# A two-layer metaformer on one core: products of ones before the first scans, layernorm sums in one PSUM bank, another conv input layout, ordered spreads and new planner keys

## The chip, the cores and the metric

The kernel runs on one core of one Trainium2 chip. The metric is device time in microseconds (us); the time before is the median of three runs. The profile is of one execution of the kernel before.

## The reference, cut to what matters

The input `x` is (8, 384, 32, 32) in float32. Two layers follow; every layernorm is without weights.

```python
# layer 0
x = x + mamba(ln_c(x))          # selective state space, 768 channels, 16 states, 1024 tokens
t = tokens(x); t = t + ffn0(ln_t(t)); x = image(t)
# layer 1
x = x + displaced_gauss(ln_c(x))  # each 8 channels shifted, then a 5x5 gaussian
t = tokens(x); t = t + ffn1(ln_t(t)); x = image(t)

def mamba(s):
    xin, z = split(s @ in_proj.T)
    u = silu(causal_conv3(xin) + conv_b)
    dt, Bm, Cm = split(u @ x_proj.T)
    dt = softplus(dt @ dt_proj.T + dt_b)
    h_t = exp(dt_t * A) * h_{t-1} + (dt_t * u_t) * B_t     # A = -exp(A_log)
    y_t = sum_n h_t * C_t + D * u_t
    return (y * silu(z)) @ out_proj.T

def ffn(x):                     # for images 0 to 4 only; zero for 5 to 7
    W = sign(W - mean) per 5 groups of output rows   # straight-through form
    h = gelu(quant(x @ W1.T + b1)); return quant(h @ W2.T + b2)
    # quant: scale by 128 / max|.| of the image and clip
```

## The kernel before, in words

One image is 1024 tokens, worked on in two halves of 512 (`s`), so the state space part has 16 units (8 images x 2 halves), `units`. Channels lie on the 128 partitions. A unit has 6 channel blocks `j` of 128, and each block has 4 state groups `g` of 4 states: 24 scan steps a unit, 384 in all.

**One scan step** (`scan`, L847 to L935): POOL multiplies the spread `dt*u` (`dus`) with B into a buffer `t` (L868, twice, 128x1024 each); ACT writes exp(dt*A) from the spread `dt` (`dts`) into PSUM (L878, four times); DVE runs four scans of 512 (L893); POOL multiplies one half by C (L914), DVE the other (L927); PE sums both over the states into the PSUM tile `y` by four products with 32 output columns each (L935). There are five buffers `t`, and PE's sum is what gives one back. `prep` makes softplus on ACT (L824) and `dt*u` on POOL (L837) for two blocks; `spread` copies each through DRAM (`via`) and back with 8 DMAs of 128 KB, which repeat each channel group over the partitions: two buffers `p`, four quarters `q` each.

**Beside the scans** lie, for the next unit, the load of x, its layernorm, the input product (`xin`, `in_proj`, L645), the three-tap convolution on DVE (L676) and `x_proj` (L760); and for units already done the output product (`end`, L997), both feed-forward nets (`ffn`, products L1386 and L1465) and `conv`, the shifted gaussian. `binarize` prepares the four weight matrices in the first part of the run (Sign on ACT at L1126). `early` makes the first layernorm and z of the last six units ahead of time.

**Layernorm** (`layernorm`, L491) is called 52 times and needs two sums over the 384 channels a call, so `total` (L458) runs 104 times. Before, `total` makes three products with a 128x32 block of ones, each into its own 32 rows of one PSUM bank (L464); ACT copies the 96 rows to SBUF (L477); and a product with `pick` (ones in one row of each 32) adds the three and spreads the sum over 128 rows (L484).

**Conv** (`conv`, L1546): per image, both halves are normalized and DVE transposes them in 32x32 blocks into `xt` (L1569); per 128 channels PE applies the vertical taps (`ups`, two products of 256 columns for each half, L1601), DVE transposes (L1615), PE applies the horizontal taps (`overs`, four products of 128 columns, L1629), DVE transposes again (L1642), and POOL adds the input (L1652). `ups` reads `xt` with 32 floats from one element to the next.

**Order.** Each step is an `op` with an engine, a planned duration and a key. `Flow.run` plays the program forward with these durations and, whenever an engine is free, takes the ready step of the lowest key (a step that needs another ACT table costs `PEN` more, and `HOLD` delays it). What comes out is a fixed order on each engine; on the chip each engine runs its own list in order and waits for semaphores. All DMAs are issued by SP in its own fixed order, and each waits for the eighth one before it. The keys are counted in scan steps: `ROWS`, `CONVS`, `K..`, `A..`, `EZ..` are shifts for parts of the work, and `UNITS` has four more for each unit (of `prep`, of the next unit's load and layernorm, of its `xin` and `x_proj`, and of `end`), all zero before.

Before, the constant `FILL` of 1e9 turns `gaps` off, which finds holes in PE's list before 45 us (`FIRST`) of the played time.

Of the kernel before, what the change touches and what calls it, by code (L numbers as in the profile page):

```python
# [36 lines left out]

KB, KE, KC_, KY, KG = -0.73, 4.53, 0.68, -3.95, -25.21  # L40

KP, KR = -4.7, 10.49
KEND, KZ, KL, KX, KXP = 1.3, 23.33, -31.97, -2.16, -4.45

KI, KJ = 196.21, 703.54
EZ, EZ0, EZ1 = 6, -56.93, 53.6

AP, AD, AA, AL = 41.75, -45.76, -50.69, -258.62

PEN = 8.61  # L50

GBS = 260.0


ROWS = [
    [15.34, -7.72, -143.06, 131.51, -3.17, 59.74, -84.96, -78.05],
    [94.3, 121.48, 131.64, -65.6, 211.87, 125.27, 265.88, 164.43],
    [164.72, 212.1, 341.92, 181.75, 145.72, 247.03, 303.52, 178.27],
    [227.6, 313.23, 335.93, 52.96, 178.3, 308.14, 239.43, 298.28],
    [299.47, 295.45, 361.88, 314.75, 306.17, 351.8, 603.44, 450.53],  # L60
]
CONVS = [
    [202.4, 111.11],
    [759.94, 953.69],
    [430.57, 41.38],
]


UNITS = [
    [0.0, 0.0, 0.0, 0.0],  # L70
    [0.0, 0.0, 0.0, 0.0],
    [0.0, 0.0, 0.0, 0.0],
    [0.0, 0.0, 0.0, 0.0],
    [0.0, 0.0, 0.0, 0.0],
    [0.0, 0.0, 0.0, 0.0],
    [0.0, 0.0, 0.0, 0.0],
    [0.0, 0.0, 0.0, 0.0],
    [0.0, 0.0, 0.0, 0.0],
    [0.0, 0.0, 0.0, 0.0],
    [0.0, 0.0, 0.0, 0.0],  # L80
    [0.0, 0.0, 0.0, 0.0],
    [0.0, 0.0, 0.0, 0.0],
    [0.0, 0.0, 0.0, 0.0],
    [0.0, 0.0, 0.0, 0.0],
    [0.0, 0.0, 0.0, 0.0],
]


# [58 lines left out]
OVER = {"PE": 0.0, "DVE": 0.085, "ACT": 0.1, "POOL": 0.05, "SP": 0.0}  # L147
TIE = 0
RUSH = -40.0
FILL, MARGIN, FIRST = 1e9, 0.8, 45.0  # L150
IDLE, COLD = 2.5, 5.0


class Flow:
# [1 line left out]


    SWITCH = 1.5
    HOLD = {"exp": 0.0, "silu": 8.77, "gelu": 2.31, "softplus": 0.0}

    def __init__(self, nc):
        self.nc, self.ops, self.key, self.filler = nc, [], 0.0, None
# [200 lines left out]
def metaformer_flow(ctx, tc, x, mw, f0, offset, f1, out):  # L363
# [24 lines left out]
    op("POOL", 2.0, lambda e: make_identity(nc, ident.ap), (), [ident])  # L388


    pick = one("pick", [P, P])

    def first_rows(e):
        e.memset(pick.ap, 0.0)
        for q in range(Q):
            e.memset(pick.ap[q * D : q * D + 1, :], 1.0)

    op("POOL", 1.0, first_rows, (), [pick])


    mm = ring("mm", [P, T], 3, ps, ordered=False)
    y_r = ring("y", [P, T], 1, ps)
# [55 lines left out]
    def total(src, acc, sq):  # L458

        def chunks(eng):
            for k in range(KC):
                eng.matmul(  # L464
                    acc.ap[k * D : (k + 1) * D, :],
                    ones.ap[:, :D],
                    src.ap[:, k, :],
                    start=True,
                    stop=True,
                    tile_position=(0, k * D),  # L470
                )

        op("PE", 1.0, chunks, [ones, src], [acc], hold=[sq])
        op(
            "ACT",
            0.6,
            lambda eng: eng.copy(sq.ap[: KC * D, 0, :], acc.ap[: KC * D, :]),  # L477
            [acc],
            [sq],
        )  # L480
        op(
            "PE",
            1.0,
            lambda eng: eng.matmul(  # L484
                acc.ap, pick.ap[: KC * D, :], sq.ap[: KC * D, 0, :], start=True, stop=True
            ),
            [pick, sq],
            [acc],
        )

    def layernorm(tn, e):  # L491

# [69 lines left out]
    def load_x(i):  # L562
# [4 lines left out]
            return  # L567
        dma(lambda: t.ap, lambda: halves(x[b], s), (), [t], 768)

    fl.key = -60  # L570
    load_x(0)
    dma(lambda: cw.ap, lambda: conv_w.rearrange("(j p) t -> p j t", p=P), (), [cw], 10)

    def small(dst, src):
# [211 lines left out]

    def spread(src, r):

        via = via_r.new()
        dma(lambda: via.ap, lambda: src.ap, [src], [via])  # L790
        dst = [r.new(Q), r.new(Q)]
        for p in range(2):
            for q in range(Q):
                dma(
                    lambda p=p, q=q: dst[p].ap[q * D : (q + 1) * D],
                    lambda p=p: via.ap.rearrange("(c d) t -> d c t", d=D)[:, 2 * p : 2 * p + 2, :],
                    [via],
                    [dst[p][q]],
                    128,
                )  # L800
        return dst

    def prep(i, a):
# [204 lines left out]
    def state_space():  # L1008
        def at(i, j, g=0.0):
            fl.key = i * UNIT + j * NG + g  # L1010

        fl.key = -50
        ln(0)
        n0 = len(fl.ops)
        for j in range(JC):
            xin(0, j)
        weights.extend([o for o in fl.ops[n0:] if o.eng == "SP"][-1:])
        x_proj(0)
        n0 = len(fl.ops)
        load_bc(0, 0)  # L1020
        fl.key = -48
        prep(0, 0)
        started.extend(o for o in fl.ops[n0:] if o.eng == "SP" and o.key == -48)
        fl.key = -46
        n0 = len(fl.ops)
        for g in range(1, NG):
            load_bc(0, g)
        fl.key = -5
        zin(0, 0)
        zin(0, 1)  # L1030
        loads.extend(o for o in fl.ops[n0:] if o.wait == 0 or o.key == -46)
        for i in range(len(units)):
            nxt = i + 1 if i + 1 < len(units) else None
            for j in range(JC):
                for g in range(NG):
                    scan(i, j, g)
                    at(i, j, g)
                    if g == NG - 1 and j % 2 and i * JC + j + 1 < len(units) * JC:
                        fl.key += KP + UNITS[i][0]
                        prep(*divmod(i * JC + j + 1, JC))  # L1040
                        at(i, j, g)
                    if j == 0 and i > 0 and g == 0:
                        fl.key += KEND + UNITS[i][3]
                        end(i - 1)
                        at(i, j, g)
                    if j == 0 and g in (0, 2):
                        fl.key += KZ
                        zin(i, 2 + g)
                        zin(i, 3 + g)
                        fl.key -= KZ  # L1050
                    if nxt:
                        if j == 1 and g == 0:
                            fl.key += KL + UNITS[i][1]
                            load_x(nxt)
                            if nxt < LATE:
                                ln(nxt)
                            at(i, j, g)
                        if j in (2, 3, 4) and g in (0, 1):
                            fl.key += KX + UNITS[i][2]
                            xin(nxt, 2 * (j - 2) + g)  # L1060
                            at(i, j, g)
                        if j == 4 and g == 2:
                            fl.key += KXP + UNITS[i][2]
                            x_proj(nxt)
                            at(i, j, g)
                        if j == JC - 1:
                            load_bc(nxt, g)
                        if j == JC - 1 and g == 1:
                            fl.key += KZ
                            zin(nxt, 0)  # L1070
                            zin(nxt, 1)
                            fl.key -= KZ
                fl.key = i * UNIT + j * NG + NG + KG
                gate(i, j)
        end(len(units) - 1)


    def binarize(w, dst, kc, o):
# [6 lines left out]
        for g in range(NQ):  # L1085
# [40 lines left out]
                lambda e, z=z, s=s: e.activation(s.ap[:, :flat], z.ap[:, :flat], AF.Sign),  # L1126
                [z],
                [s],
            )
            op(  # L1130
                "POOL",
# [414 lines left out]
    def conv(src, dst, dst_ap):  # L1546

        xt = [hb_r.new(2) for _ in range(KC)]
        for s in range(NS):
# [14 lines left out]
            for c in range(KC):  # L1564
# [2 lines left out]
                    "DVE",  # L1567
                    0.7,
                    lambda e, c=c, tn=tn, ys=ys: e.transpose(  # L1569
                        xt[c].ap.rearrange("p (y c) -> p y c", c=32)[:, ys, :],  # L1570
                        tn.ap[:, c, :].rearrange("p (y x) -> p y x", x=32),
                    ),
                    [tn],
                    [xt[c][s]],
# [1 line left out]
        for c in range(KC):  # L1576
# [18 lines left out]
            for h in range(2):  # L1595
                acc = mm.new()

                def ups(e, lt=lts[0], acc=acc, h=h, c=c):
                    for k in (0, 1):
                        cs = slice(h * 16 + k * 8, h * 16 + k * 8 + 8)  # L1600
                        e.matmul(  # L1601
                            acc.ap.rearrange("p (c y) -> p c y", y=32)[:, k * 8 : k * 8 + 8, :],
                            lt.ap[:, 2 * h + k, :],
                            xt[c].ap.rearrange("p (y c) -> p c y", c=32)[:, cs, :],
                            start=True,
                            stop=True,
                        )

                op("PE", 1.0, ups, [lts[0], xt[c]], [acc], hold=[tr])
                hs = slice(h * T, (h + 1) * T)  # L1610

                op(
                    "DVE",
                    0.7,
                    lambda e, tr=tr, acc=acc, hs=hs: e.transpose(  # L1615
                        tr.ap[:, hs].rearrange("p (c x) -> p c x", x=32),
                        acc.ap.rearrange("p (c y) -> p c y", y=32),
                    ),
                    [acc],
                    [tr[h]],  # L1620
# [1 line left out]
            for h in range(2):  # L1622
# [3 lines left out]
                def overs(e, lt=lts[1], acc=acc, xs=xs, tr=tr):  # L1626
# [7 lines left out]
                            stop=True,  # L1634
                        )

                op("PE", 1.3, overs, [lts[1], tr], [acc])

                op(
                    "DVE",  # L1640
                    0.85,
                    lambda e, c=c, acc=acc, xs=xs: e.transpose(  # L1642
                        xt[c].ap.rearrange("p (x y) -> p x y", y=32)[:, xs, :],
                        acc.ap.rearrange("p (c x) -> p x c", x=16),
# [3 lines left out]
                )  # L1648
            op(
                "POOL",  # L1650
                2.35,
                lambda e, xr=xr, c=c: e.tensor_add(  # L1652
                    xr.ap.rearrange("p (y x) -> p y x", x=32),
                    xr.ap.rearrange("p (y x) -> p y x", x=32),
# [106 lines left out]
```

## Time and profile before

| | |
|---|---|
| median of 3 runs | 3707.25 us (3698.68 to 3713.39) |
| profiled execution | 3705.44 us; its span 3703.7 us |
| mean granted TensorE clock | 0.923 |
| PE busy | 3189.1 us (86%) |
| POOL busy | 3157.0 us (85%) |
| DVE busy | 3086.6 us (83%) |
| ACT busy | 2494.7 us (67%) |

The page gives busy time by engine, the span in 40 slices, the chain of work that ended last, and the costliest groups. A float32 product is two matmul instructions in the profile, so its counts are twice those of the code. Ends of matmuls are modelled, and the busy time of PE holds their latency, so PE is less full than its share says.

### The profile page before, as it was taken

What the parts mean: (1) busy time and instruction counts of PE and PEld (TensorE: products, weight loads), DVE (VectorE), ACT (ScalarE), POOL (GpSimd) and SP (SyncE); (2) the same over time, 40 slices, a digit from 0 to 9 for tenths busy, and PEclk for the clock granted to TensorE, in tenths of its full rate; (3) what the DMA queues carried; (4) which work ended last, traced back from release to release, by engine and by line L of the source; (5) the groups of instructions that cost most, each with busy time, mean ns of one, the idle gap of its engine ahead of it and who ended that gap; (6) DMA issues with size and microseconds to landing.
All of it is one profiled execution on the core that took longest, in us unless ns stands there. A gap on an engine that the chain in (4) does not pass through costs nothing.

```text
span 3703.7 us, 35888 instructions
## 1 busy us (share of the span) xinstructions
PE 3189.1 (86%) x9572; PEld 1143.7 (31%) x9572; DVE 3086.6 (83%) x3080; ACT 2494.7 (67%) x3661; POOL 3157.0 (85%) x1680
## 2 busy tenths in 40 slices
PE   4777878987999897899979789998877999878988
PEld 1222223322333231333323233332223333323334
DVE  2798888878778889997987899889898888788986
ACT  4767886757667676677768757767665676765562
POOL 3879999897697998888899887989998788997893
PEclk7888979998999897999989899999988999988999
DMA  5858778696686886668587776969776787976964
GB/s 145 184 154 223 198 199 221 184 256 181 207 245 175 231 224 181 200 199 243 177 248 205 196 221 193 244 198 255 228 216 195 209 246 225 257 217 207 270 185 155
DMA packets 680820, 777.44 MB, mean 210 GB/s; under 512 B 113689, under 2 KB 434089, under 8 KB 680617
## 3 DMA queue, kind: packets, MB, share of 16 engines
q1 hardware_dynamic: 680616, 775.14, 74.4%
q8 instruction: 77, 1.26, 0.1%
q14 instruction: 127, 1.03, 0.1%
HBM read 578.45 MB, written 196.48 MB: 209 GB/s over the span
## 4 chain that ended last, share of the span: by engine, by line
PE 39%; DVE 16%; DMA 15%; POOL 12%; ACT 10%; issue 6%; SPq 2%; POOLq 0%; DVEq 0%; ACTq 0%
PE mm L1386 10%; PE mm L1465 9%; POOL t L868 8%; PE mm L645 6%; DVE dp L893 5%; PE y L935 4%; DMA dus<-via 3%; PE mm L997 3%; DVE t L893 3%; POOL t L914 3%; DVE t L927 3%; DMA dts<-via 2%; ACT L359 2%; ACT dp L878 2%; PE mm L1601 2%
## 5 line engine op out<-in xcount | busy, mean ns | idle before, releaser
L868 POOL TENSOR_TENSOR t<-dus,bc 128x1024 f32<-128x1024 f32 x768 | 1797.8, 2361 | 209.9 <-PE y L935 169.6
L914 POOL TENSOR_TENSOR t<-t,bc 128x1024 f32<-128x1024 f32 x384 | 906.8, 2362 | 99.6 <-DVE t L893 89.6
L935 PE MATMUL y<-t,sel 128*32 128x512 f32 x3072 | 554.9, 652 | 184.4 <-DVE t L927 117.8
L1465 PE MATMUL mm<-hb,w 128*128 128x512 f32 x1440 | 675.4, 609 | 28.4 <-DMA w<-w2d 12.1
L1386 PE MATMUL mm<-tn,w 128*128 128x512 f32 x1440 | 670.9, 611 | 24.7 <-DMA w<-w1d 7.5
L878 ACT ACTIVATE da<-dts,aneg 128x512 f32<-128x512 f32 x768 | 520.6, 684 | 240.7 <-DVE t L893 216.0
L878 ACT ACTIVATE dp<-dts,aneg 128x512 f32<-128x512 f32 x768 | 528.3, 688 | 207.2 <-DVE t L927 190.3
L893 DVE TENSOR_TENSOR_SCAN dp<-dp,h,t 128x512 f32<-128x512 f32 x384 | 491.3, 1279 | 71.7 <-ACT dp L878 53.5
L893 DVE TENSOR_TENSOR_SCAN dp<-dp,t 128x512 f32<-128x512 f32 x384 | 468.4, 1220 | 90.6 <-ACT dp L878 59.8
L893 DVE TENSOR_TENSOR_SCAN t<-da,h,t 128x512 f32<-128x512 f32 x384 | 481.2, 1267 | 64.2 <-POOL t L868 59.6
L893 DVE TENSOR_TENSOR_SCAN t<-da,t 128x512 f32<-128x512 f32 x384 | 458.2, 1206 | 79.5 <-POOL t L868 68.5
L359 ACT ACT_TABLE_LOAD x391 | 501.7, 1283 | 6.5
L645 PE MATMUL mm<-xn,win 128*128 128x512 f32 x900 | 439.3, 631 | 39.6 <-DMA win<-in_L_conv_in_proj_w 20.5
L927 DVE TENSOR_TENSOR t<-dp,bc 128x1024 f32<-128x1024 f32 x384 | 465.4, 1212 | 8.8 <-ACT h L920 4.0
L1465 PEld LDWEIGHTS mm<-hb,w 128*128 128x128 f32 x1440 | 264.9, 192 | 431.8 <-issue 352.7
L1386 PEld LDWEIGHTS mm<-tn,w 128*128 128x128 f32 x1440 | 269.4, 193 | 413.8 <-issue 311.5
L997 PE MATMUL mm<-z,wo 128*128 128x512 f32 x552 | 276.6, 634 | 12.2 <-DMA wo<-in_L_conv_out_proj_w 7.6
L645 PEld LDWEIGHTS mm<-xn,win 128*128 128x128 f32 x900 | 173.6, 200 | 294.7 <-issue 209.7
L1398 ACT ACTIVATE he<-mm,b 128x512 f32<-128x512 f32 x240 | 162.9, 680 | 148.9 <-PE mm L1386 141.6
L935 PEld LDWEIGHTS y<-t,sel 128*32 128x32 f32 x3072 | 83.4, 112 | 560.0 <-DVE t L927 201.1
L920 ACT COPY h<-dp 128x2 f32<-128x2 f32 x192 | 30.5, 159 | 218.4 <-DVE t L927 112.6
L1408 DVE TENSOR_REDUCE sm<-he 128x1 f32<-128x1024 f32 x120 | 144.3, 1203 | 30.8 <-ACT he L1398 30.2
(133 smaller groups left out, 3170.5 us busy)
## 6 DMA issues: line engine op xcount, KB each, us to landing
dts<-via SPq DMA_DIRECT2D x768, 128.0 KB, 4.4
dus<-via SPq DMA_DIRECT2D x768, 128.0 KB, 4.5
hd<-he SPq DMA_DIRECT2D x120, 512.0 KB, 4.7
hb<-hd SPq DMA_DIRECT2D x120, 512.0 KB, 5.9
via<-soft SPq DMA_DIRECT2D x192, 256.0 KB, 4.3
w<-w2d SPq DMA_DIRECT2D x120, 384.0 KB, 4.7
w<-w1d SPq DMA_DIRECT2D x240, 192.0 KB, 3.9
bc<-bcd SPq DMA_DIRECT2D x256, 128.0 KB, 4.7
```

What stands on the lines that cost most here:

```text
L359: nc.scalar.preload_act_table_set(SETS[table])
L645: e.matmul(acc.ap, w.ap[:, k, :], xn.ap[:, k, :], start=(k == 0), stop=(k == KC - 1))
L868: lambda e, t=t, du=du: e.tensor_mul(t.ap, du.ap, wide(0)),
L878: lambda e, c=c, r=r, dt=dt: e.activation(decay(c), dt.ap[:, r, :], AF.Exp, scale=aneg.ap[:, j * Q + c, g : g + 1],),
L893: e.tensor_tensor_scan(t.ap[:, r, :] if p == 0 else decay(c), decay(c), t.ap[:, r, :], 0.0 if s == 0 else hst[j][p].ap[:, g, r : r + 1], A ...
L914: op("POOL", 2.35, lambda e, t=t: e.tensor_mul(t.ap, t.ap, wide(1)), [bc], [t])
L927: lambda e, t=t: e.tensor_mul(t.ap, da[2].ap, wide(1)),
L935: e.matmul(y.ap[c * D : (c + 1) * D, :], sel.ap, ts[c // 2].ap[:, c % 2, :], start=(g == 0), stop=(g == NG - 1), tile_position=(0, c * D),)
L997: e.matmul(o.ap, flat()[:, j, :], zs[j].ap, start=(j == 0), stop=(j == JC - 1))
L1386: e.matmul(acc.ap, w.ap[:, k, :], tn.ap[:, k, :], start=(k == 0), stop=(k == KC - 1),)
L1398: lambda e, he=he, r=r, m=m, acc=acc: e.activation(he.ap[:, r, :], acc.ap, AF.Identity, bias=b1.ap[:, m : m + 1]),
L1465: e.matmul(acc.ap, w.ap[:, part * 2 + r, :], hs[m // 2].ap[:, r * T : (r + 1) * T], start=(m == 0), stop=(m == MC - 1),)
```

## The change

1. `FILL` becomes 1.0. Wherever PE's list has a hole of 1 us or more before 45 us of the played time, products of ones with ones, 256 columns each, are put in, into a bank of the ring `mm` that is free then; nothing reads them. In the order that comes out they are 29: 6 before the first layernorm sum, 8 before the second, 12 before the first input product and 3 before the fourth.
2. `total` becomes three products with the full 128x128 block of ones that add up in one PSUM bank. ACT's copy and `pick` with its POOL memsets are gone. Its planned duration is 1.83 us.
3. In `conv` the transposed input is laid out in four blocks of (row, 8 channels), so `ups` reads 256 floats in a row; DVE writes in runs of eight, and L1615 reads in the matching order. Some planned durations change (`ups` 1.0 to 0.75, `overs` 1.3 to 1.2, L1642 0.85 to 0.7, the POOL add 2.35 to 2.85).
4. `spread` gives keys in the order dts p0, dus p0, dts p1, dus p1.
5. The load of the first x goes ahead of the small loads (key -62).
6. The Sign activations of `binarize` ask for the table "exp"; before they asked for none.
7. All keys change, `UNITS` gets values, `PEN` and `HOLD` change.

```diff
-KB, KE, KC_, KY, KG = -0.73, 4.53, 0.68, -3.95, -25.21
+KB, KE, KC_, KY, KG = -0.44, 5.96, 0.99, -3.06, -26.35
...
-PEN = 8.61
+PEN = 12.76
...
 UNITS = [
-    [0.0, 0.0, 0.0, 0.0],
...
+    [2.22, 11.11, 13.63, -1.02],
+    [5.11, 17.35, 2.38, 1.26],
...
-FILL, MARGIN, FIRST = 1e9, 0.8, 45.0
+FILL, MARGIN, FIRST = 1.0, 0.8, 45.0
...
-    pick = one("pick", [P, P])
-
-    def first_rows(e):
-        e.memset(pick.ap, 0.0)
-        for q in range(Q):
-            e.memset(pick.ap[q * D : q * D + 1, :], 1.0)
...
         def chunks(eng):
             for k in range(KC):
-                eng.matmul(
-                    acc.ap[k * D : (k + 1) * D, :],
-                    ones.ap[:, :D],
-                    src.ap[:, k, :],
-                    start=True,
-                    stop=True,
-                    tile_position=(0, k * D),
-                )
-
-        op("PE", 1.0, chunks, [ones, src], [acc], hold=[sq])
-        op(
-            "ACT",
-            0.6,
-            lambda eng: eng.copy(sq.ap[: KC * D, 0, :], acc.ap[: KC * D, :]),
...
-            lambda eng: eng.matmul(
-                acc.ap, pick.ap[: KC * D, :], sq.ap[: KC * D, 0, :], start=True, stop=True
-            ),
...
+                eng.matmul(acc.ap, ones.ap, src.ap[:, k, :], start=(k == 0), stop=(k == KC - 1))
+
+        op("PE", 1.83, chunks, [ones, src], [acc], hold=[sq])
...
+    fl.key = -62
+    load_x(0)
     fl.key = -60
-    load_x(0)
...
-        via = via_r.new()
+        via, k0 = via_r.new(), fl.key
...
         for p in range(2):
+            fl.key = k0 + 0.02 * p + (0.01 if r is dus_r else 0.0)
...
                 lambda e, z=z, s=s: e.activation(s.ap[:, :flat], z.ap[:, :flat], AF.Sign),
                 [z],
                 [s],
+                table="exp",
...
-                        xt[c].ap.rearrange("p (y c) -> p y c", c=32)[:, ys, :],
-                        tn.ap[:, c, :].rearrange("p (y x) -> p y x", x=32),
+                        xt[c].ap.rearrange("p (k y c) -> p y k c", k=4, c=8)[:, ys],
+                        tn.ap[:, c, :].rearrange("p (y a b) -> p y a b", a=4, b=8),
...
-                        cs = slice(h * 16 + k * 8, h * 16 + k * 8 + 8)
                         e.matmul(
-                            acc.ap.rearrange("p (c y) -> p c y", y=32)[:, k * 8 : k * 8 + 8, :],
+                            acc.ap[:, k * 256 : k * 256 + 256],
                             lt.ap[:, 2 * h + k, :],
-                            xt[c].ap.rearrange("p (y c) -> p c y", c=32)[:, cs, :],
+                            xt[c].ap[:, (2 * h + k) * 256 : (2 * h + k + 1) * 256],
```

The filler is `keep`, which stood in the kernel before already:

```python
    def keep(e, b):
        e.matmul(b[:, : 2 * P], ones.ap, ones.ap.unsqueeze(1).to_broadcast([P, 2, P]), start=True, stop=True)
```

## The prediction

> **What bounds the kernel now.** I read the page first (busy shares, chain, costliest groups), then the waits, then the groups with what ended their idle time, then the timeline of the first 100 us and of the end. Each line of the groups has busy us, mean ns of one, then idle time before and what ended it.
>
> ```profile
> PE 3189.1 (86%) x9572; PEld 1143.7 (31%) x9572; DVE 3086.6 (83%) x3080; ACT 2494.7 (67%) x3661; POOL 3157.0 (85%) x1680
> ...
> PE 39%; DVE 16%; DMA 15%; POOL 12%; ACT 10%; issue 6%; SPq 2%; POOLq 0%; DVEq 0%; ACTq 0%
> ...
> L868 POOL TENSOR_TENSOR t<-dus,bc 128x1024 f32<-128x1024 f32 x768 | 1797.8, 2361 | 209.9 <-PE y L935 169.6
> ...
> L359 ACT ACT_TABLE_LOAD x391 | 501.7, 1283 | 6.5
> ```
>
> No engine is full. POOL and DVE are nearly so, and POOL's largest loss is 169.6 us at L868, where it waits for a buffer t that PE's sum L935 gives back. The chain runs over PE for 39% of the span, over ACT for 10%: it is the place in PE's list, not PE's total, that costs. So a microsecond added to PE is worth about 0.39 us, one taken from ACT 0.10.
>
> The groups that the change touches, and one of each kind that replaces them:
>
> ```profile
> L464 PE MATMUL mm<-sq,ones 128*32 128x512 f32 x312 | 64.2, 691 | 34.9 <-ACT sq L512 30.7 <-ACT tail L663 2.8 <-ACT soft L824 0.8
> ...
> L477 ACT COPY sq<-mm 96x512 f32<-96x512 f32 x104 | 60.1, 577 | 64.9 <-PE mm L464 61.6 <-PE y L935 1.5 <-ACT soft L824 0.6
> ...
> L484 PE MATMUL mm<-sq,pick 96*128 96x512 f32 x208 | 128.3, 702 | 39.5 <-ACT sq L477 37.9 <-ACT h L920 1.5
> ...
> L1601 PE MATMUL mm<-hb,lt 128*128 128x256 f32 x192 | 89.2, 615 | 13.0 <-DVE hb L1569 8.4 <-DVE hb L1642 4.1 <-DVE xn L498 0.5
> ```
>
> And the timeline (start, length): a full-width chain of three products, a sum in its two parts, and both forms of conv product late in the run; then the start.
>
> ```profile
> 3514.52 2.84 PE L1386 MATMUL mm<-tn,w 128*128 128x512 f32 x6
> ...
> 3652.43 1.06 PE L464 MATMUL mm<-xn,ones 128*32 128x512 f32 x6
> ...
> 3654.41 1.02 PE L484 MATMUL mm<-sq,pick 96*128 96x512 f32 x2
> ...
> 3692.46 3.04 PE L1629 MATMUL mm<-hb,lt 128*128 128x128 f32 x24
> ...
> 3688.92 3.71 PE L1601 MATMUL mm<-hb,lt 128*128 128x256 f32 x8
> ```
>
> ```profile
> 5.20 0.55 SPq L217 DMA_DIRECT2D xn<-in_x  x1
> ...
> 10.87 1.93 PE L464 MATMUL mm<-xn,ones 128*32 128x512 f32 x6 [10.87 <-DMA xn<-in_x]
> ...
> 26.88 4.75 PE L645 MATMUL mm<-xn,win 128*128 128x512 f32 x6 [3.21 <-DVE xn L537]
> ...
> 34.04 2.74 PE L645 MATMUL mm<-xn,win 128*128 128x512 f32 x6
> ...
> 78.64 4.64 POOL L868 TENSOR_TENSOR t<-dus,bc 128x1024 f32<-128x1024 f32 x2
> ...
> 97.92 9.26 POOL L868 TENSOR_TENSOR t<-dus,bc 128x1024 f32<-128x1024 f32 x4 [8.90 <-DMA bc<-bcd]
> ```
>
> Before 98 us POOL does little: the scans wait for one chain from x to the spreads. At its head the products run at half speed (4.75 us for what takes 2.74 later).
>
> **Start: -4 us.** The x load is now SP's first: issued near 0.74, where the first DMA was, and 5.7 us later in, near 6.4 instead of 10.87. The ones are ready near 1.9 (the five pick memsets are gone), so six fillers, at 0.43 us an instruction of 256 columns while slow, hold PE until about 7.0 and cost 0.6. If PE is then at full speed, the first sum ends at 9.8, the DVE step (1.76) and the square (1.48) at 13.2, the second sum at 16.0, Ln, the small aneg step and Exp (0.66, 0.28, 0.58) at 17.6, the DVE step (1.75) at 19.5. The twelve fillers after the second sum are 24 instructions of 0.21, 5.1 us, and end near 20.9: 1.4 past the hole. The input product starts at 20.9 instead of 26.88 and runs fast: the first block is 8.1 earlier. Then ACT leads (about 2.9 us a block), and there the new table for Sign costs: in ACT's order an exp load and a silu load now stand before the last silu but one (2.57), and another load before the copy that precedes the softplus (1.28). Left: 8.1 - 3.9 = 4.2. In the order of spreads, eight DMAs instead of sixteen stand before the first scan; they were issued over 10 us, so the first L868 comes another 3 us earlier, near 71. But the steady flow begins with the bc loads at 97.92, whose place behind all spreads is the same, and the DMAs are busy there (0.83 of their time between 51 and 102 us). So 4, bounds 0 (all taken back by these DMAs) and 8.
>
> [...] The row at 26.88 rose after some 4 us, so I keep the warm case.
>
> **Layernorm sums: +79 us on PE, -60 on ACT, -38 of PE's waiting.** 104 sums. By the timeline one had 1.06 + 1.02 on PE, and 3.0 us from end to end; it becomes a chain like L1386, 2.84. PE gets 0.76 x 104 = 79 more. The group rows say less (260.5 us for L464 and L484 together against 624 x 0.466 = 291: +30); I take 79, since the groups hold the slow start. ACT loses 60.1, and PE no longer stands 37.9 us waiting for the copy. The latency of a layernorm hardly moves.
>
> **Conv: -43 us on PE, 0 on DVE.** L1629 takes 1.0 us for 1024 columns (3.04 for 24 instructions of 128), L1601 1.85 for the same number (3.71 for 8 of 256): the difference is the stride of 32 floats. Read in a row, `ups` should cost as `overs`: 0.9 x 48 = 43 saved; bound 0 if it is not the read. DVE's writes get shorter runs, its L1615 reads strides. L1642 already reads at a stride of 16 and takes 692 ns in its group, against 677 for L1569, so 0; bound +34 (L1569 twice as long, times 48). POOL's add keeps its layout; 2.35 to 2.85 is only the planner's number.
>
> **Tables: +18 us on ACT.** ACT's list holds 410 loads against 396: 14 x 1.283.
>
> Sum for the 3530 us between: PE +79 - 43 - 38 = -2 at 0.39, ACT -60 + 18 = -42 at 0.10: -5 us. Bounds: if the 37.9 was idle that costs nothing, +10; with +30 for the sums, -24.
>
> **Spreads in order: -3 us.** ACT waits 5.0 and 11.5 us for dts in the groups of L878, POOL 8.6 for dus: 25 in all, of which I take an eighth; bounds 0 and -25. SP's lists hold equally many DMAs.
>
> **End: -3 us.** After the last L927 (3632) one layernorm and three channel blocks of conv stand alone; two sums gain 0.2 each, `ups` some 0.9 in each of three blocks: 3.1; bounds 0 and -6.
>
> **Keys: 0, the widest bound.** Nearly every row of every list moves. I cut both orders into stretches of scan steps and summed each engine's work with the rows' durations. Taking the fullest of DVE, POOL and PE in each stretch, 96 stretches of 4 steps give 3582 before and 3614 after, 16 stretches of 24 steps 3337 and 3321. So the balance is the same: +32 to -16, and I take 0. What this can't see is in which moment a sum L935 stands behind a chain; the 169.6 us above are the stake.
>
> The profiled execution took 3705.4, 1.8 under the median. -4 - 5 - 3 - 3 = -15: 3690 for it; against the median 3692.
>
> **Rivals.** *(B) The order frees the t buffers.* If the new places of L935 take back a third of the 169.6 us, 57 more go: 3635; half of that, 3663. For: PE has room, being partly idle. Against: equal balance. *(C) The start is hidden and conv's read isn't the cost*: -4 and -17 (43 x 0.39) fall away: 3692 + 21 = 3713, no change. *(D) Slower: sums longer than planned hold up L935.* The planner reckons 1.83 for what takes 2.84, so PE falls behind its plan by 1.0 x 104 = 105 us, in front of L935 sums that were placed to the microsecond, and POOL stands at L868. At 0.39 that is 41, in full 105: 3733 to 3797 (the sum's own 79 is inside). It decides if the t buffers have no reserve when a layernorm is in PE's list; for it speaks that 169.6, against it that before `ups` was under-planned alike (1.0 for 1.85, 48 times).
>
> **The numbers.** The sum stands: 0.46, own range 3672 to 3711. B 0.24, C 0.10, D 0.20. About 0.5% (18.5 us) can be told from no change, so faster ends at 3688.7: B, and 0.20 of the 0.46, as the sum lies 3 us above: 0.44. Same: 0.26 and C: 0.36. Slower: D, 0.20. The range: 3640 to 3740 leaves out a fourth of B (0.06) and more than half of D (0.12).
>
> **What would show it.** Right: the first sum near 7 with 2.6 to 2.8 us, the input product near 21, the first L868 near 71 and steady POOL near 94; L464 near 290 busy, no L477; `ups` near 45; L868's idle behind L935 within 30 of 169.6. Wrong: that wait over 210 (D) or under 120 (B); products still slow at 9 us; `ups` still at 89.

## The result, and the profile after

| kernel | median | runs |
|---|---|---|
| before | 3701.47 us (3698.68 to 3713.39) | 7 |
| changed | 3725.26 us (3709.09 to 3739.46) | 7 |

The ratio is 1.006 [1.0038, 1.0082]: slower by 0.6%, 22 us. The forecast was 3692 with 3640 to 3740 around it: the time lies in the range, on the other side of no change. The profiled execution took 3722.73 us (span 3720.8). In all that follows "us against before" is (ratio - 1) x 3702.

Line numbers shift with each edit: in the changed kernel L868 is L838, L935 is L905, L464 is L454, L645 is L613 and L1601 is L1571. From the page after (busy shares, then groups: busy us, mean ns, idle before and what ended it):

```profile
PE 3215.6 (86%) x9422; PEld 1213.3 (33%) x9422; DVE 3085.5 (83%) x3080; ACT 2464.6 (66%) x3571; POOL 3154.3 (85%) x1675
...
L838 POOL TENSOR_TENSOR t<-dus,bc 128x1024 f32<-128x1024 f32 x768 | 1795.8, 2358 | 221.7 <-PE y L905 177.8
...
L359 ACT ACT_TABLE_LOAD x409 | 524.7, 1283 | 6.7
```

The instructions went as announced: PE 150 fewer, ACT 30 us less busy, 14 more table loads (410, one of them at another line, against 396). PE is busy 26.5 us more, and POOL's wait for a buffer t behind the sum over y grew by only 8 (169.6 to 177.8). The shares of the chain that ended last add up to 3% here and can't be read.

The groups of PE that the change touched:

```profile
L454 PE MATMUL mm<-sq,ones 128*128 128x512 f32 x312 | 162.9, 663 | 47.7 <-ACT sq L479 38.6 <-ACT h L890 7.0 <-ACT tail L631 1.2
L454 PE MATMUL mm<-tn,ones 128*128 128x512 f32 x246 | 130.6, 672 | 29.5 <-DMA tn<-x 18.4 <-DVE tr L1506 5.0 <-DMA tn<-in_x 3.4
L454 PE MATMUL mm<-xn,ones 128*128 128x512 f32 x66 | 35.2, 677 | 7.0 <-ACT dp L848 5.0 <-DMA xn<-in_x 1.9
...
L1571 PE MATMUL mm<-hb,lt 128*128 128x256 f32 x192 | 55.8, 434 | 17.5 <-DMA lt<-ltd 5.4 <-DVE hb L1540 5.2 <-DVE hb L1585 2.8
```

The sums are 328.7 us busy, 68 more than their two parts (260.5; foreseen: near 290, and 79 more). `ups` is at 434 ns where it was at 615: its stride did cost. The start, in the timeline (start, length, idle before):

```profile
1.96 5.49 PE L397 MATMUL mm<-ones 128*128 128x256 f32 x12 [1.96 <-POOL sm L1119]
7.24 2.94 PE L454 MATMUL mm<-xn,ones 128*128 128x512 f32 x6
10.02 3.62 PE L397 MATMUL mm<-ones 128*128 128x256 f32 x16
13.55 2.84 PE L454 MATMUL mm<-sq,ones 128*128 128x512 f32 x6
16.23 5.34 PE L397 MATMUL mm<-ones 128*128 128x256 f32 x24
22.73 2.84 PE L613 MATMUL mm<-xn,win 128*128 128x512 f32 x6 [1.16 <-DVE xn L504]
```

```profile
16.50 0.66 ACT L488 ACTIVATE mm<-mm,eps 128x512 f32<-128x512 f32 x1 [1.70 <-PE mm L454]
20.12 0.28 ACT L585 ACTIVATE aneg<-aneg 128x96 f32<-128x96 f32 x1 [2.96 <-DMA aneg<-in_L_conv_A_log]
20.31 0.58 ACT L496 ACTIVATE mm<-mm 128x512 f32<-128x512 f32 x1
```

PE is warm from the first sum on: the fillers ahead of it took 0.46 us an instruction, those behind it 0.23 and 0.22, and the three chains 2.94, 2.84 and 2.84 us. But in ACT's list the small aneg step stands between Ln and Exp, and its load lands only at 20.1: the input product comes at 22.73, not 20.9.

What became of the start is seen in where each scan step begins. I took the start of the first scan of every step from the traces and subtracted that of before (one profiled execution of each kernel; those named e are told below):

```
scan step          1     4     7    10    13    25   193   384
changed         -6.7   0.2   7.1  19.3  13.8  13.4  22.6  23.7
e6             -10.1  -6.2  -0.2  12.3   6.7   5.8  20.1  22.3
e7              -7.2  -0.6   6.5  17.5  11.9  11.2  -5.1 -16.3
e9              -4.0  -6.8  -6.8  -6.8  -7.2  -9.6   3.8  13.2
e10             -5.4  -9.2  -8.6  -9.1  -7.6 -10.3  -9.5 -20.6
e5              -3.6  -7.4  -7.4  -7.4  -8.2  -8.8  -8.4  -0.5
e2              -0.4  -4.8  -4.8  -4.8  -5.8  -6.7  -0.4  -8.4
```

The lead of 6.7 us at the first scan is gone at the fourth step, and at the tenth the changed kernel is 19 behind. The last row tells how far one trace can be trusted: e2 differs from before only in the conv, whose first product starts at 866 us of before, and still lies 5 to 7 us ahead from the fourth to the 25th step (0.4 at the first scan). Behind the first scan, smaller shifts than that aren't read. PE's timeline in that stretch, before and then after:

```profile
110.71 2.74 PE L723 MATMUL mm<-tn,w 128*128 128x512 f32 x6
113.28 2.74 PE L645 MATMUL mm<-xn,w 128*128 128x512 f32 x6
...
116.44 1.42 PE L935 MATMUL y<-t,sel 128*32 128x512 f32 x7
117.80 1.13 PE L484 MATMUL mm<-sq,pick 96*128 96x512 f32 x2
118.85 1.13 PE L814 MATMUL mm<-dbc,wdt 24*128 24x512 f32 x4
119.91 1.07 PE L935 MATMUL y<-t,sel 128*32 128x512 f32 x8
```

```profile
112.15 1.07 PE L905 MATMUL y<-t,sel 128*32 128x512 f32 x8
113.14 2.84 PE L613 MATMUL mm<-xn,win 128*128 128x512 f32 x6
115.82 2.74 PE L613 MATMUL mm<-xn,w 128*128 128x512 f32 x6
118.40 2.74 PE L691 MATMUL mm<-tn,w 128*128 128x512 f32 x6
120.97 2.74 PE L613 MATMUL mm<-xn,win 128*128 128x512 f32 x6
123.55 2.74 PE L691 MATMUL mm<-tn,w 128*128 128x512 f32 x6
126.22 1.06 PE L905 MATMUL y<-t,sel 128*32 128x512 f32 x8
```

After, five chains stand between two sums over y, 13 us without a pause, and POOL waits for that sum (2.85 us here). From 110 to 125 us, before and then after (length; busy PE, PEld, DVE, ACT, POOL; granted clock, DMA share, GB/s):

```profile
110.00:125.00 15.00, 11.82 (x44) 3.99 (x43) 12.13 (x10) 14.71 (x22) 12.76 (x8) 0.93 0.95 287
```

```profile
110.00:125.00 15.00, 15.00 (x42) 6.23 (x41) 9.48 (x8) 14.16 (x21) 10.14 (x7) 1.00 0.82 255
```

PE is full (15.00 of 15 us), at full clock (1.00 granted), and DVE and POOL work 5 us less between them. ACT is nearly full in both (14.71 and 14.16 us). Between 95 and 170 us POOL's waits for PE's y were 1.5 us before and are 13.9 now:

```profile
POOL t L838 <- PE y L905: 13.9, 4, 5.3
```

DVE's waits for ACT grew more, from 6 us to 24. The largest, before and then after:

```profile
DVE dp L893 <- ACT dp L878: 3.6, 3, 2.2
DVE tn L537 <- ACT mm L529: 2.0, 1, 2.0
```

```profile
DVE dp L863 <- ACT dp L848: 10.4, 2, 6.7
DVE t L863 <- ACT mm L488: 5.1, 1, 5.1
DVE tn L504 <- ACT mm L496: 4.7, 1, 4.7
DVE t L897 <- ACT h L890: 4.1, 2, 2.9
```

So the scans are held up by the places of steps in the lists of both PE and ACT; which of the two leads, these waits don't say.

### The profile page after: what moved, and what is told of

Read it like the earlier page. It is cut to its first block, busy times and chain, and to the rows that moved or that the text cites. A ratio compares the mean times of both kernels' runs of the same rounds, so it can differ in the third digit from the quotient of the medians.

```text
span 3720.8 us, 35429 instructions
## 1 busy us (share of the span) xinstructions
PE 3215.6 (86%) x9422; PEld 1213.3 (33%) x9422; DVE 3085.5 (83%) x3080; ACT 2464.6 (66%) x3571; POOL 3154.3 (85%) x1675
## 5 line engine op out<-in xcount | busy, mean ns | idle before, releaser
L838 POOL TENSOR_TENSOR t<-dus,bc 128x1024 f32<-128x1024 f32 x768 | 1795.8, 2358 | 221.7 <-PE y L905 177.8
L1436 PE MATMUL mm<-hb,w 128*128 128x512 f32 x1440 | 685.1, 616 | 60.6 <-ACT hb L1412 27.8
L905 PE MATMUL y<-t,sel 128*32 128x512 f32 x3072 | 524.8, 646 | 186.3 <-DVE t L897 101.8
L1357 PE MATMUL mm<-tn,w 128*128 128x512 f32 x1440 | 659.8, 603 | 25.1 <-DVE tn L504 8.1
L613 PE MATMUL mm<-xn,win 128*128 128x512 f32 x900 | 429.3, 618 | 22.7 <-DMA win<-in_L_conv_in_proj_w 8.4
L613 PEld LDWEIGHTS mm<-xn,win 128*128 128x128 f32 x900 | 170.6, 197 | 269.8 <-issue 202.3
L905 PEld LDWEIGHTS y<-t,sel 128*32 128x32 f32 x3072 | 75.5, 111 | 548.3 <-DVE t L897 173.1
L454 PE MATMUL mm<-sq,ones 128*128 128x512 f32 x312 | 162.9, 663 | 47.7 <-ACT sq L479 38.6
```

What stands on the lines that cost most here:

```text
L454: eng.matmul(acc.ap, ones.ap, src.ap[:, k, :], start=(k == 0), stop=(k == KC - 1))
L613: e.matmul(acc.ap, w.ap[:, k, :], xn.ap[:, k, :], start=(k == 0), stop=(k == KC - 1))
L838: lambda e, t=t, du=du: e.tensor_mul(t.ap, du.ap, wide(0)),
L905: e.matmul(y.ap[c * D : (c + 1) * D, :], sel.ap, ts[c // 2].ap[:, c % 2, :], start=(g == 0), stop=(g == NG - 1), tile_position=(0, c * D),)
L1357: e.matmul(acc.ap, w.ap[:, k, :], tn.ap[:, k, :], start=(k == 0), stop=(k == KC - 1),)
L1436: e.matmul(acc.ap, w.ap[:, part * 2 + r, :], hs[m // 2].ap[:, r * T : (r + 1) * T], start=(m == 0), stop=(m == MC - 1),)
```

## The experiments

Theory P: what PE has more to do in layernorm's sums costs, in any order. Theory K: the new order costs, whatever the operations; keys and the planner's numbers are fitted to one another. D is the prediction's rival: the sums are planned too short. The results, each against before in the same comparison:

| kernel | median us | ratio | us |
|---|---|---|---|
| e1 sums alone, order before | 3721.45 | 1.005 [1.0032, 1.0068] | +18.5 |
| e2 conv alone, order before | 3693.30 | 0.9975 [0.9961, 0.9989] | -9 |
| e3 changed, keys of before | 3786.72 | 1.0231 [1.021, 1.0252] | +86 |
| e4 before, new keys | 3809.45 | 1.0298 [1.0272, 1.0324] | +110 |
| e5 unread products alone | 3697.42 | 0.9987 [0.9973, 1.0001] | -5 |
| e6 changed, no table for Sign | 3719.31 | 1.0054 [1.0037, 1.0071] | +20 |
| e7 changed, two products in a sum | 3682.77 | 0.9956 [0.994, 0.9972] | -16 |
| e8 conv and start, order before | 3690.05 | 0.9971 [0.9958, 0.9984] | -11 |
| e9 all parts, order before | 3705.15 | 1.0009 [0.9993, 1.0024] | +3 |
| e10 as e9, two products in a sum | 3683.45 | 0.9949 [0.9936, 0.9962] | -19 |
| e11 changed, truer durations planned | 3791.69 | 1.0242 [1.0226, 1.0258] | +90 |
| e12 before, one truer duration planned | 3782.46 | 1.0218 [1.0198, 1.0239] | +81 |

**e1: the sums alone, in the order before.** The chain stands where the first part stood; the copy and the pick issue nothing.

```diff
-                eng.matmul(acc.ap[k * D : (k + 1) * D, :], ones.ap[:, :D], src.ap[:, k, :], ...)
+                eng.matmul(acc.ap, ones.ap, src.ap[:, k, :], start=(k == 0), stop=(k == KC - 1))
...
-            lambda eng: eng.copy(sq.ap[: KC * D, 0, :], acc.ap[: KC * D, :]),
+            lambda eng: None,
```

> The kernel before with its order of every engine kept; only the sums are made the new way (three full-width products into one bank in the first PE slot, nothing emitted for the copy on ACT and the product with pick). Theory K (the new keys' order costs the time, the parts gain): 3695 to 3703, as PE's +79 and the lost waiting of 38 nearly cancel. Theory P (the longer sums hold up PE's list whatever the order is): +15 to +40, so 3717 to 3742, with POOL's wait on PE's sum over the states (169.6 before) above 185.

+18.5 us. Its page:

```profile
PE 3236.8 (87%) x9364; PEld 1204.4 (32%) x9364; DVE 3086.6 (83%) x3080; ACT 2444.4 (66%) x3557; POOL 3157.5 (85%) x1680
...
L845 POOL TENSOR_TENSOR t<-dus,bc 128x1024 f32<-128x1024 f32 x768 | 1797.9, 2362 | 223.4 <-PE y L912 191.3
```

(L845 and L912 are L868 and L935 of before.) ACT has 50 us less, PE no longer waits 37.9 us for the copy, and the kernel is slower: POOL waits 22 us more for the sum over y (169.6 to 191.3), about the whole loss. Theory P holds.

**e2: the conv layout alone, in the order before.** The edits of `xt` and `ups` only.

> The kernel before with its order kept; only the conv input is laid out in runs of eight. Both theories: the vertical products fall from 89 to about 50 us busy, the time by 5 to 20 us (43 us of PE at 0.39). If the layout costs DVE more than it saves PE, the transposes grow above 0.75 us each and the time stays at 3701 or rises.

-9 us, for 29 us less of PE (3189.1 to 3159.9). `ups`, and the DVE transposes that touch the new layout, in its groups:

```profile
L1600 PE MATMUL mm<-hb,lt 128*128 128x256 f32 x192 | 56.5, 437 | 14.2 <-DVE hb L1569 7.6 <-DVE hb L1641 4.7 <-DVE xn L537 0.8
...
L1614 DVE STREAM_TRANSPOSE hb<-mm 128x512 f32<-128x512 f32 x48 | 33.2, 700 | 12.5 <-PE mm L1600 11.9
...
L1569 DVE STREAM_TRANSPOSE hb<-tn 128x512 f32<-128x512 f32 x45 | 28.6, 681 | 0.5 <-POOL hb L1651 0.5
```

Before, these were 615 ns for `ups` and 706 and 677 for the two transposes.

**e3 and e4: the keys without the parts, and the parts without the keys.** In both the planner makes a new order.

```diff
 # e3: the changed kernel
-KB, KE, KC_, KY, KG = -0.44, 5.96, 0.99, -3.06, -26.35
+KB, KE, KC_, KY, KG = -0.73, 4.53, 0.68, -3.95, -25.21
...
-PEN = 12.76
+PEN = 8.61
 # and so on for every key, UNITS and HOLD; e4 is the reverse, on the kernel before
```

> The changed kernel with the keys of before (UNITS zero, old PEN and HOLD): all structural parts, planned anew. Theory K: 3680 to 3700, faster than both. Theory P: 3715 to 3740, like the changed kernel, since the sums are in it.

> The kernel before with the new keys, UNITS, PEN and HOLD alone, planned anew. Theory K: 3720 to 3750, the loss of the whole change plus what the parts gained. Theory P: 3690 to 3710, no loss without the longer sums.

+86 and +110 us, beyond every range that was expected of either theory. The waits of POOL (us in total, times, longest) in e3, then in e4:

```profile
POOL t L838 <- PE y L905: 162.8, 93, 9.4
POOL t L884 <- DVE t L863: 131.1, 54, 10.0
POOL h L880 <- DVE t L863: 121.4, 52, 6.4
```

```profile
POOL t L868 <- PE y L935: 241.3, 105, 25.8
POOL h L910 <- DVE t L893: 99.0, 47, 6.0
```

In e4 POOL waits 72 us more behind the sum over y; in e3 that wait is even shorter than before, and POOL waits for DVE's scans instead (252 us in the two rows, 164 before). So the keys are far from neutral: each set does much better with the steps and durations it came with, and the new one brings the changed kernel from +86 to +22.

**e5: the unread products alone, in the order before.**

```diff
-FILL, MARGIN, FIRST = 1e9, 0.8, 45.0
+FILL, MARGIN, FIRST = 1.0, 0.8, 45.0
...
-                    if now - idle >= IDLE and (now > FIRST or FILL > 1e6):
+                    if now - idle >= IDLE:
```

> The kernel before in its own order, with only the 26 unread products added in PE's idle stretches ahead of the first scan (8, 8, 7 and 3 of them); x is still loaded where it was. Theory S (the start is on the path: what the first scan gains, the end gains): the first layernorm's sums and the first input product run at full speed, the input product 2.7 to 2.9 us instead of 4.75, the first scan 3 to 4 us earlier than 78.6, and the end 2 to 4 us earlier: 3699 to 3701. Theory H (the steady flow begins with the bc transfers, whatever PE did): the first scan 3 to 4 earlier, the second not, and the end within 1.5 of before: 3702 to 3704.

-5 us, with an interval from -10 to 0. The input product takes 2.74 us and the first scan comes 3.6 earlier. The tenth step comes 7.4 earlier and the last one 0.5, but e2, whose start is untouched, is 4.8 ahead at the tenth step too. The median is below the ranges of both theories: a small gain is likely, that it is what the first scan won is not shown.

**e6: the changed kernel, Sign without a table of its own.** Three loads leave ACT's list (410 to 407), nothing else moves.

> The changed kernel in its own order, but Sign in the first input blocks asks for no table of its own, as in the kernel before: three table loads fewer in ACT's list, all ahead of the first scans; nothing else moves. The prediction took 3.9 us for them in the sum of the start. If they are on the path: the first scan 3.5 to 4 us earlier than 74.3, and the end 2 to 4 earlier than the changed kernel: 3721 to 3723. If what was won at the start is lost anyway to the order of the scan steps that follow (by step 8 the lead of 6.7 us was gone): the first scan 3.5 to 4 earlier, the end within 2 of the changed kernel.

The first scan is 3.4 us earlier than in the changed kernel, the seventh 7.3, the last 1.4 (table above); the medians differ by 2 us, less than their intervals. The price at the start was right (3.9 foreseen), and the end doesn't see it.

**e7: the changed kernel with two products in a sum.**

```diff
-            for k in range(KC):
-                eng.matmul(acc.ap, ones.ap, src.ap[:, k, :], start=(k == 0), stop=(k == KC - 1))
+            for k in range(KC - 1):
+                eng.matmul(acc.ap, ones.ap, src.ap[:, k, :], start=(k == 0), stop=(k == KC - 2))
```

> The changed kernel in its own order, with two of the three products in each layernorm sum: a third of the channels is left out of the sums, PE has 208 products and some 97 us less, and every sum ends 0.95 us earlier. Theory P (the longer sums are what the change lost; by the sum alone in the order before, 15 us of wait for 47.7 us of PE, 0.32 a microsecond): 97 x 0.32 = 31 earlier, 3690 to 3700, and the wait of POOL for a t buffer behind the sum over y falls from 177.8 to about 150. Theory K (the new order itself costs some 20 us against the order before, and PE's load is covered in it): within 8 of the changed kernel, 3717 to 3727, wait 170 to 180. Between, 3703 to 3714: each has a part, in the proportion of the distance.

From +22 to -16: 38 us for some 97 of PE (208 products of 0.466), 0.40 a microsecond. Theory P, and more than it asked:

```profile
PE 3138.4 (85%) x9214; PEld 1176.2 (32%) x9214; DVE 3080.8 (84%) x3080; ACT 2465.1 (67%) x3571; POOL 3154.8 (86%) x1675
...
L838 POOL TENSOR_TENSOR t<-dus,bc 128x1024 f32<-128x1024 f32 x768 | 1797.5, 2362 | 190.8 <-PE y L905 145.4
```

The wait behind the sum over y falls by 32 us, most of the gain. The first steps are as late as with three products (17.5 at the tenth); the gain comes afterwards.

**e8: the parts that gain, in the order before.** The layout of e2, the unread products of e5, and the x load sorted to the head of SP's list.

> The order before with the parts of the change that should gain: the first input of the convolution in runs of eight, the unread products at the start, and x loaded by SP's first DMA; layernorm's sums stay in their two parts. By the convolution alone, -10 us; by the start in the changed kernel, where the first scan came 6.7 us earlier, -4 to -7 if it is kept in an order that was made for these steps. Sum: 3686 to 3690 if the start is kept to the end, 3691 to 3694 if it is lost on the way. Above 3700 would say that the order tolerates neither.

-11 us: the lowest time of the kernels that leave nothing out, ahead of both, though e2 alone is within its interval. But the x load brought nothing. The unread products before the first sum are too many for it (timeline of PE):

```profile
3.19 5.97 PE L408 MATMUL mm<-ones 128*128 128x256 f32 x16 [3.19 <-POOL sm L1151]
9.09 1.06 PE L466 MATMUL mm<-xn,ones 128*32 128x512 f32 x6
10.83 1.13 PE L486 MATMUL mm<-sq,pick 96*128 96x512 f32 x2 [0.69 <-ACT sq L479]
```

The first sum begins at 9.09, straight behind them, where the changed kernel began at 7.24; its second sum's pick then waits 3.9 us for ACT, and the first scan comes 3.3 earlier, no more than in e5. Against e2 the time is 1 to 2 us lower, less than the intervals, so what the start is worth to the end isn't shown here either.

**e9: all parts, in the order before.** e1 and e8 together.

> All the parts of the change (layernorm sums as one chain, the convolution's first input in runs of eight, unread products at the start, x loaded first) on the order before: its keys, planned durations and spreads. If the parts simply add up as they did alone: +18 for the sums, -11 for the convolution with the start, so some 3706 to 3712, and the changed kernel's 3725 then owes 13 to 19 to its new order. If the parts are worth less together than alone and the order costs nothing: 3720 to 3728.

+3 [-3, +9]: the parts add up (18.5 - 11 = 8 was expected), and the changed kernel, with the same parts, is 19 us slower (1.006 against 1.0009; about 10 either way by the two intervals). That is what its order costs: keys, planned numbers, ordered spreads, and with them Sign's tables (e6) and the places of the unread products (29 against 26). The profiled execution of e9 lies 16 us above its median and within 2 us of the changed kernel's, so its late shifts in the table are not read, and these two traces can't show where the 19 us lie. The early shifts are read: 7 us ahead at the tenth step, where the changed kernel is 19 behind. Sign's tables don't make that difference, for e6 is 12 behind.

**e10: as e9, with two products in a sum.**

> As the kernel with all parts on the order before, with two of the three products in each layernorm sum: a third of the channels is left out of the sums, and PE has 208 products and some 97 us less. In the changed kernel the same edit took 42 us, 0.43 a microsecond. If the price belongs to PE's load in any order (theory P): 31 to 42 below the kernel with three, 3668 to 3678. If the old order has more room around its sums than the new one: 10 to 25 below. A sum of two products takes PE 1.9 us where the two parts of before took 2.08 without their wait: so this kernel against the one with the convolution and start alone (3690) shows what the copy on ACT and the wait of 38 us ahead of the pick were worth: 3668 to 3678 would mean 12 to 22, near the 21 that the prediction gave them; 3688 to 3692 nothing.

22 us less than e9, 0.23 a microsecond of PE; in the new order it was 0.40. With the short sums the two orders are equal (0.9949 and 0.9956), though e7 is still 17.5 us behind at the tenth step where e10 is 9 ahead: what the new order loses there can be made up. So the new order may be the more sensitive to the sums' length; the difference of 16 us between the two effects is little more than the intervals together (12), and I leave it at that. Against e8, which has the sums in two parts, e10 has 17 us less of PE (3168.5 to 3151.3), 51 less of ACT (2494.9 to 2443.6) and no wait for the copy, and gains 8 us, 7 either way.

**e11 and e12: truer numbers for the planner.** e11 tells the changed kernel's planner 2.65 us for a sum (1.83 in the change) and 0.95 for `ups` (0.75); the 2.85 for the add stands there already. e12 changes one number in the kernel before, POOL's add:

```diff
                 "POOL",
-                2.35,
+                2.85,
                 lambda e, xr=xr, c=c: e.tensor_add(
```

> The changed kernel with its planner told durations nearer to those measured: a layernorm sum 2.65 instead of 1.83, the convolution's first product 0.95 instead of 0.75, POOL's add 2.85. The same work, in an order planned anew with the same keys. Theory D (the changed kernel loses because its planner reckons the sums too short, and POOL waits behind them): faster than the changed kernel by 10 to 40, 3685 to 3715. Theory K (keys and plan are tuned to each other, and any new order away from that point loses): slower by 20 to 100, 3745 to 3825.

> The kernel before, with one planned duration set nearer to what its trace shows: POOL's add in the convolution reckoned at 2.85 instead of 2.35 us, 24 times. No operation is added, removed or changed, only the order that the planner makes of them after the first third of the lists. Theory K (the keys are tuned to the very order that the plan gave): slower by 15 to 100, 3716 to 3800. If an order planned with the truer number is as good as another: 3690 to 3712.

+90 and +81 us, with the same operations but for table loads; the changed kernel lost 68 by its planner's knowing better. e12's waits:

```profile
POOL t L868 <- PE y L935: 205.3, 85, 30.6
POOL h L910 <- DVE t L893: 91.2, 40, 9.0
...
POOL he L1344 <- DVE sm L1337: 40.4, 3, 39.8
```

One add, 24 times in the run, reckoned half a microsecond longer: POOL's wait behind the sum over y grows by 36 us, and one wait at L1344 near the end is 40 where it was 26. Theory K holds, in this sense: with given keys each of the four other plans made here (e3, e4, e11, e12) loses 2 to 3%. As a cure for D, truer numbers are shown wrong here; as the cause of the changed kernel's loss, too short sums are neither shown nor excluded, since every new plan brings the loss of a new plan.

## Why the prediction was wrong

**Failed: "Keys: 0".** The forecast summed each engine's work over stretches of scan steps and found the balance unchanged; it said that it could not see where a sum over y stands behind a chain. That was the largest term: against e9 the new order, with what goes with it, costs 19 us (about 10 either way), within the bounds of -16 to +32. How it does so is shown in part only. In the first twelve scan steps all three kernels of the new order fall behind (at the thirteenth the changed kernel is 14 behind before, e6 7, e7 12, while e9 is 7 ahead): between 95 and 170 us POOL waits 12 us more for the sum over y, and DVE 18 more for ACT. But e7 falls behind as far and ends level with e10, so this early loss need not be the 19 us, and whether the order costs them by itself or only with the longer sums stays open. What the forecast had at stake, POOL's wait behind the sum over y, doesn't follow the time from one order to another: 177.8 us in the changed kernel, 185.4 in e9, and 151.9 in e11 at +90. A balance over stretches didn't price the order; e3, e4, e11 and e12 show what one can cost with nearly the same work.

**Failed: the layernorm sums' waiting.** The body's sum took +79 and -38 of PE at 0.39 and -60 of ACT at 0.10: +10 us for the sums. Measured were +18.5 (e1) and +14 (e9 against e8). The error is in the 38 us of waiting for the copy, which the forecast credited like busy time: 27 us would be due to e10 against e8 by its factors (17 x 0.39, 51 x 0.10, 38 x 0.39), and 8 came. Of 126 us that PE stood idle ahead of the sums and picks, 96 remain in e1; that nothing POOL needs was late while PE stood there is the likely reason, not a shown one. The +79 itself at 0.39 was fair (0.23 and 0.40 a microsecond by e10 and e7; by the page PE's busy time falls by 72 and 77, not 97, which makes 0.31 and 0.50). That the price fits is luck in part: it is the share of one chain, and the same view gives PE 9% in e2, with the same order, and 3% in the changed kernel.

**Conv: right in cause, too large.** -43 on PE became -33 (89.2 to 55.8; foreseen 45), and -17 us became -9 (e2): 0.32 a microsecond. DVE's transposes did not notice the layout: 701 and 694 ns at L1585 and L1612 (706 and 692 before), 679 at L1540 (677).

**Start: right at the first scan, lost at once.** The first sum at 7.24 (near 7 foreseen), warm (2.94 us); the first L838 at 71.95 (near 71), the steady flow at 92.64 (near 94). For the warm case spoke the row at 26.88 of before: there the weight loads came 0.85 us apart up to 30.46 and 0.43 us apart from 31.04 on, so after some 4 us of products. Here 5.49 us of fillers stood ahead of the first sum; how few would do is not shown. A slow product behind fillers did occur in e9: there they end at 20.26, PE stands 2.44 us, and the first input product takes 4.54 us, at a granted clock of 0.50 between 23.5 and 26.7. Missed was that aneg's load would stand before Exp: 2.96 us of ACT's wait in the row at 20.12. The first input block was done 6 us earlier, not 8.1, so the hit at the first scan is in part luck. Of "Sign: 3.9" 3.4 was measured (e6). The -4 may be of the right size for a kept order (-5 in e5, interval -10 to 0); in the changed one the lead was gone at the fourth step.

**Spreads and end.** The -3 for the spreads can't be told from the order around them: no run moved them alone. The end after the last scan is 6.5 us shorter in the changed kernel (17 behind at the end, 24 at the last scan), but by 0.5 only in e8 with the same conv layout: it seems to be the order's, not the shorter `ups`.

**Tables.** 14 more loads, 18 us of ACT. Between 100 and 135 us, where the lead is lost, there are 8 against 6 before and in e9: two loads of 1.28 us are little of it, though where the loads stand in ACT's list is part of the order; e6, without the first three, loses the lead too.

**The rivals.** B, the freed buffers, fell: the wait grew. The sign that was to show the sum right, a wait within 30 of 169.6, came true in a slower kernel. D had the direction and the sensitivity (e7: 38 us hang on the sums' length), but not the mark that it named, over 210 us behind L935; the wait is 177.8. Of C's two grounds one fell (the read was the conv's cost), and the other, a hidden start, came true in the changed kernel.

The forecast was 15 us below before, the result is 22 above it. Of these 37, some 20 are thus the order (19 measured, -1 foreseen for spreads and tables), 4 to 8 the sums, 8 the conv and 3 the end, each of the measured ones with 5 to 10 us either way.

## What to carry to other kernels

When a change replans an order that is written out ahead and was tuned, the plan can be the largest term, as here: price it by putting the same parts into the old order (e9) before believing any sum of parts, and don't expect truer planner numbers to help without new keys (e11, e12). Count a wait of an engine as a gain only if someone waits for what is behind it: 38 us of waiting, 51 us of ACT and 17 of PE were together worth 8, 7 either way, while 97 us of PE's work in the layernorm sums were worth 22 to 38. A lead at the start is not yet a gain: 6.7 us at the first scan were gone at the fourth step. And before reading shifts of a few microseconds from one trace, see how far two traces of the same instructions lie apart (5 to 7 us here).

## What the runs showed of the hardware

Three products into 32 columns of their own took 1.06 us together (before, at 3652.43), where the chain of three takes 2.84 (changed, at 13.55), 2.7 times as long; this change gave that up for one copy and the product with `pick` less. A moving operand at a stride of 32 floats cost `ups` 615 ns an instruction against 434 in a row, 33 us over 192 instructions; a DVE transpose that reads at a stride of 16 floats took 692 ns (L1642), those that read in a row 677 (L1569) and 706 (L1615), and at a stride of 8 it took 701 (L1585, the L1615 of before).
